# Keeping the masks of layer 0 on chip for layer 1 in a two-layer graph network kernel

## The chip, the cores and the metric

The kernel runs on one core of one Trainium2 chip. The metric is the device time of one execution in microseconds (us), the median of three runs. The core has five engines that run side by side and are tied together by semaphores: TensorE (in the profile PE, and PEld for its weight loads), VectorE (DVE), ScalarE (ACT), GpSimd (POOL) and SyncE (SP), which here only issues transfers. Sixteen DMA engines move the data that the queues of SP, ACT and POOL ask for.

## The reference

Sixteen graphs of 1024 nodes with 256 features each, and an adjacency matrix of integers (about 3% ones, ones on the diagonal). Layer 0 is masked attention with 8 heads of 32 features, layer 1 an attention over edge scores; both have a layer norm in front and a residual around them.

```python
# layer 0
h = jnp.maximum(_layernorm(x), 0.0)
Q, K, V = proj(Wq, bq), proj(Wk, bk), proj(Wv, bv)          # 8 heads of 32
scores = jnp.where(adj[:, None] == 0, -jnp.inf, Q @ K.T * SCALE)
x = x + (softmax(scores) @ V).reshape(b, n, 256) @ Wo.T + bo
# layer 1
h = jnp.maximum(_layernorm(x), 0.0)
scores = jnp.where(adj == 1, leaky_relu((h * a_0) @ h.T), NEG_INF)
...
scores = jnp.where(adj == 4, leaky_relu((h * a_3) @ h.T), scores)
x = x + softmax(scores) @ h
```

With the inputs drawn here adj holds only 0 and 1, so for layer 1 only a_0 matters. A path for other values (`layer_1_of_kinds`) stands at the end behind a test and isn't entered.

## The kernel before

A graph is worked through in 8 tiles of 128 query rows. The main loop (L710) runs over *steps*, one tile of layer 0 each: 128 tiles and ten more steps until the pipeline is empty. A step has 8 *slots*, one for each head (`h`, L713). In one step four tiles are under way:

- `now` (class `Attend`): the tile whose heads are scored. In slot h TensorE makes the scores (L402), VectorE adds the mask and takes the maximum in one pass (L414), ScalarE takes the exponential one slot later (L422), and the probabilities are turned two slots later. Odd heads are turned by TensorE and copied by ScalarE (L514, L515); even heads are turned by VectorE in blocks of 32 (L347), and four transfers of 128 KB on SP's queue put the blocks in place (L352).
- `was`: the tile before. In slot 3 `combine(1)` multiplies its heads 4 to 7 with the values (L457); heads 0 to 3 were done in slot 7 of its own step (`combine(0)`). Then output, residual, norm, and in slot 6 the result goes to DRAM (`keep`, L486).
- `edge`, `edge_was` (class `Edges`): a tile of layer 1 that lies `LAG` = 9 steps back. Scores in slots 0 and 1 (L543), maximum in slot 2 (L556), leak in 3 (L564), exponential in 4 (L568), blocks in 5 and 6, gathered (L584) and stored (L594) in the step after that.
- `piece`, `piece_was` (class `Piece`): a tile nine steps ahead, whose norm, queries, keys and values are made. Its keys go to DRAM twice: once on SP's queue as they are made (slots 0 and 1) and once on POOL's queue (`write_again`, slot 1, L297). At a change of graph the eight key tiles of the next graph, 512 KB each, are loaded on POOL's queue (`load_key`, L331), one in each slot from slot 3 of a graph's last step to slot 2 of the next graph's first.

Each engine and each queue works in the order in which the program writes its instructions; nothing is reordered. SP's order in a full step is: slot 0, keys of the piece, blocks of head 6 of the tile before; slot 1, keys, the next tile's adjacency (`Attend.load`, L376), its queries (L372); slot 2, blocks of head 0; slot 3, the next piece's nodes (L192) and the next edge tile's adjacency (`Edges.load`, L525); slot 4, blocks of head 2, and the residual of the edge tile (L572); slot 6, queries of the piece (L291), blocks of head 4, `keep`, the residual of the tile (`load_nodes`, L380), the edge tile's blocks; slot 7, the output.

POOL turns an adjacency tile into a mask of bf16 twice: for `Attend` (L384, slot 3) and, nine steps later, for `Edges` (L537, slot 7). Besides it has the chains of small operations of the norm (L144 to L160; slots 1 and 5), the spread reciprocals (L441, slot 1), the bias (L388, slot 2) and the scaled rows `ha` of layer 1 (L530, slot 4). ScalarE squares the adjacency tile in place once, to find whether it holds other kinds (`flag`, L393, slot 0).

The rows of an `Attend` tile are dealt to the partitions in another order than in DRAM (`mixed`, L341: row b*32+k lies on partition k*4+b), and those of an `Edges` tile in the order of DRAM. So `keep` stores through `mixed`, and `Edges` loads straight.

Of the kernel before, what the change touches and what calls it, by code (L numbers as in the profile page):

```python
# [17 lines left out]
P = 128  # L18
HEADS = 8
# [23 lines left out]
def gnn_kernel(  # L43
# [26 lines left out]
    LEAD = NT + 1  # L70

# [99 lines left out]
    class Piece:  # L171
# [5 lines left out]
        def __init__(self, b, first, n=1):  # L177
            self.b, self.first, self.n = b, first, n
            self.cols = slice(first * P, (first + n) * P)
            self.projected, self.halved, self.again = [], [], []  # L180
            self.tags = ("xin", "h0", "hT", "halves", "hTm") if n == 1 else ("adj", "pT", "qt", "p", "blocks")

        def buffer(self, i, shape, dtype=F32, bufs=2):
# [3 lines left out]
            bufs = {"p": 4, "blocks": 3}.get(tag, bufs)  # L187
# [75 lines left out]
        def high(self):  # L263
            which, oc, ps, bias = self.projected.pop(0)
            halves = self.buffer(3, [P, 2 * self.n * P], F32R, 4)
# [36 lines left out]
        def write_again(self):  # L302
            for oc, halves in self.again:
                self.write_keys(oc, halves, nc.gpsimd, 1)
# [39 lines left out]

    def blocks_of(p):
# [12 lines left out]
    h1s, h1Ts, x1ds = {}, {}, {}  # L358
    kinds_seen = const.tile([P, B * NT], F32, name="kinds_seen")

    class Attend:

# [11 lines left out]
        def load(self):  # L374
            self.adj = work.tile([P, N], I32, tag="adj")
            nc.sync.dma_start(out=self.adj, in_=mixed(adj[self.b, self.rows, :]))  # L376

        def load_nodes(self):
            self.xb = work.tile([P, D], F32, tag="xb")
            nc.sync.dma_start(out=self.xb, in_=mixed(x[self.b, self.rows, :]))  # L380

        def mask(self):
            self.neg = work.tile([P, N], BF16, tag="neg")
# [81 lines left out]
        def combined(self):  # L465
            self.oT = work.tile([P, NC, P], F32, tag="oT")
# [9 lines left out]
        def residual(self):  # L476
            self.x1 = work.tile([P, D], F32, tag="x1")
# [5 lines left out]
        def keep(self):  # L483
            if self.t == 0:
                x1ds[self.b] = dram.tile([N, D], F32, tag=f"x1d{self.b}", name=f"x1d_{self.b}", bufs=1)
            nc.sync.dma_start(out=mixed(x1ds[self.b][self.rows, :]), in_=self.x1)  # L486
# [31 lines left out]
    class Edges:  # L518
# [4 lines left out]
        def load(self):  # L523
            self.adj = work.tile([P, N], I32, tag="adj")
            nc.sync.dma_start(out=self.adj, in_=adj[self.b, self.rows, :])  # L525

        def prepare(self):
            self.ha = work.tile([P, NC, P], F32, tag="ha")
            for c in range(NC):
                nc.gpsimd.tensor_scalar(  # L530
                    self.ha[:, c], h1Ts[self.b][:, c, self.rows], a_t[:, c, 0:1], 0.0, ALU.mult, ALU.add
                )

        def mask(self):
            self.neg = work.tile([P, N], BF16, tag="neg1", bufs=1)

            nc.gpsimd.tensor_scalar(self.neg, self.adj, 0.0, MASKED, ALU.is_equal, ALU.mult)  # L537
# [14 lines left out]

        def softmax_max(self):
# [3 lines left out]
                out=self.sel, in0=self.e, in1=self.neg, scale=-1.0, scalar=3e38,  # L557
# [8 lines left out]
        def softmax_exp(self):  # L566
# [4 lines left out]
            self.x1 = work.tile([P, D], F32, tag="x1b")  # L571
# [17 lines left out]
        def store(self):  # L589
            rec = small.tile([P, 1], F32, tag="rec1")  # L590
            nc.vector.reciprocal(rec, self.total)
            ot = work.tile([P, D], F32, tag="ot")
            nc.vector.scalar_tensor_tensor(ot, sums_place, rec, self.x1, ALU.mult, ALU.add)  # L593
            nc.sync.dma_start(out=out[self.b, self.rows, :], in_=ot)  # L594


    def layer_1_of_kinds(b):
        h1 = graph.tile([P, NT, D], F32, tag="h1", name=f"h1g_{b}")
        h1T = graph.tile([P, NC, N], F32, tag="h1T", name=f"h1Tg_{b}")
        for t in range(NT):  # L600
            rows = slice(t * P, (t + 1) * P)
            xt = work.tile([P, D], F32, tag="x1")
            nc.sync.dma_start(out=xt, in_=x1ds[b][rows, :])
# [8 lines left out]
        for t in range(NT):  # L612
            rows = slice(t * P, (t + 1) * P)
            at = work.tile([P, N], I32, tag="adj")
            nc.sync.dma_start(out=at, in_=adj[b, rows, :])
            xt = work.tile([P, D], F32, tag="x1b")
            nc.sync.dma_start(out=xt, in_=x1ds[b][rows, :])

            code = work.tile([P, N], BF16, tag="neg1", bufs=1)
# [3 lines left out]
            for k in range(N_KINDS):  # L623
                ha = work.tile([P, NC, P], F32, tag="ha")
# [4 lines left out]
                is_k = work.tile([P, N], U16, tag="neg")  # L629
# [23 lines left out]
            ot = work.tile([P, D], F32, tag="ot")  # L653
# [20 lines left out]
    with tc.manual_schedule():  # L674
# [8 lines left out]
        now, piece_next = attend_of(0), piece_of(0)  # L683
        now.load()
        now.load_nodes()
        now.mask()
        piece_next.load()
# [22 lines left out]
        for s in range(B * NT + LAG + 1):  # L710
            b, t = divmod(s, NT)
            nxt, edge_nxt, piece_nxt = attend_of(s + 1), edges_of(s + 1), piece_of(s + 1)
            for h in range(HEADS):  # L713
# [41 lines left out]
                if h == 0:  # L755
                    if edge:
# [4 lines left out]
                    if now:  # L761
                        now.flag()
                if h == 1:
# [8 lines left out]
                    if nxt:  # L772
                        nxt.load()
# [8 lines left out]
                if h == 3:  # L782
                    if was:
                        was.combine(1)
                    if piece_nxt:
# [112 lines left out]
```

## Time and profile before

| | |
|---|---|
| median of 3 runs | 3405.14 us (3405.12 to 3412.75) |
| the profiled execution | 3404.83 us, its span 3403.0 us |
| TensorE clock granted, mean | 0.978 of full speed |
| moved by DMA | 830.24 MB, 244 GB/s over the span |
| transfers of blocks (L352) | 2560 of 128 KB, 3.3 us to landing (median) |
| adjacency loads (L376 and L525) | 256 of 512 KB, 5.3 us to landing |
| key loads on POOL's queue (L331) | 120 of 512 KB, 7.1 us to landing |
| POOL making masks | 128 x 3653 ns (L384) and 128 x 3659 ns (L537) |

How to read the lines that follow. A group shows line, engine, operation, output<-input, and how often. A line of waits reads "engine, line, what it waited for: us in total, times, longest". In the order of time the first two numbers are the start and the time until the end of the last of a run of equal instructions; in square brackets stands the idle time before and what ended it. SPq is SP's queue: its lines are issues of transfers, and their time is that of issuing. "To landing" runs from the issue of a transfer to the arrival of its last byte. A busy TensorE isn't TensorE at its peak, since ends of matmuls are modelled; idle time of an engine that isn't the bound costs nothing.

### The profile page before, as it was taken

The numbers are of one execution on the slowest core, as the hardware profiler recorded it, in microseconds if no ns is written. First come the engines' busy times: TensorE is split into PE (matmuls) and PEld (weight loads), VectorE is DVE, ScalarE is ACT, GpSimd is POOL, SyncE is SP. The second block draws the span as 40 slices with busy tenths as digits, with TensorE's granted clock in tenths as the row PEclk, the third lists the DMA queues.
The fourth block names the chain that finished last, engine by engine and source line by source line (L and its number), as shares of the span: only waits on it lengthen the run. The fifth ranks groups of instructions, "written<-read, shape, count | busy, mean of one in ns | idle before, by whom it ended". The sixth has DMA issues, their size and how long they took to land. (4 is left out here: it accounts for less than half of the span.)

```text
span 3403.0 us, 100938 instructions
## 1 busy us (share of the span) xinstructions
PE 3126.6 (92%) x36018; PEld 2247.9 (66%) x36018; DVE 2788.1 (82%) x5111; ACT 2418.2 (71%) x4829; POOL 2432.1 (71%) x5634
## 2 busy tenths in 40 slices
PE   5879989999999989999899999999999999998988
PEld 3666767666676767766666676767666676666653
DVE  3878888788888888888788788888888888788874
ACT  2887767677777777777777677777777677776751
POOL 2567777777777777777777777777777777776553
PEclk7999999999999999999999999999999999999999
DMA  6787788888888788788878888888788888888664
GB/s 221 211 249 241 234 268 249 268 239 245 265 241 277 236 268 247 237 271 248 267 231 250 265 236 282 240 270 248 234 268 249 267 235 251 267 238 261 196 175 113
DMA packets 802029, 830.24 MB, mean 244 GB/s; under 512 B 73840, under 2 KB 742640, under 8 KB 801520
## 3 DMA queue, kind: packets, MB, share of 16 engines
q1 hardware_dynamic: 769520, 725.10, 71.3%
q0 software_dynamic: 28800, 94.39, 7.9%
q8 instruction: 291, 4.77, 0.5%
q10 hardware_dynamic: 3200, 4.19, 0.3%
q14 instruction: 218, 1.79, 0.1%
HBM read 320.08 MB, written 167.77 MB: 143 GB/s over the span
## 5 line engine op out<-in xcount | busy, mean ns | idle before, releaser
L422 ACT ACTIVATE p<-p,nmx 128x1024 f32<-128x1024 f32 x1024 | 1179.2, 1152 | 454.9 <-DVE nmx L414 450.9
L414 DVE CUSTOM_DVE_ANT_0 p<-s,neg 128x1024 f32<-128x1024 f32 x1024 | 1242.1, 1213 | 207.2 <-PE s L402 195.8
L402 PE MATMUL s<-k,qt 128*128 128x512 f32 x2048 | 794.5, 469 | 41.3 <-DMA k<-kd 14.8
L457 PE MATMUL acc<-pT,v 128*32 128x128 f32 x16384 | 576.3, 283 | 140.2 <-DMA pT<-blocks 136.6
L515 ACT COPY pT<-trp 128x512 f32<-128x512 f32 x1024 | 542.5, 580 | 136.1 <-PE trp L514 134.6
L347 DVE STREAM_TRANSPOSE blocks<-p 128x1024 f32<-128x1024 f32 x512 | 634.8, 1240 | 0.0
L457 PEld LDWEIGHTS acc<-pT,v 128*32 128x32 f32 x16384 | 476.1, 113 | 213.6 <-issue 204.4
L514 PE MATMUL trp<-ident,p 128*128 128x128 f32 x4096 | 534.0, 274 | 2.1 <-ACT p L422 2.0
L514 PEld LDWEIGHTS trp<-ident,p 128*128 128x128 f32 x4096 | 480.7, 141 | 75.1 <-ACT p L422 6.9
L384 POOL TENSOR_SCALAR neg<-adj 128x1024 bf16<-128x1024 int32 x128 | 467.6, 3653 | 78.8 <-DMA adj<-in_adj 69.8
L584 PE MATMUL acc<-h,pT 128*32 128x256 f32 x8192 | 505.8, 383 | 6.2 <-DMA pT<-blocks 5.5
L537 POOL TENSOR_SCALAR neg<-adj 128x1024 bf16<-128x1024 int32 x128 | 468.4, 3659 | 39.0 <-DMA adj<-in_adj 29.0
L402 PEld LDWEIGHTS s<-k,qt 128*128 128x128 f32 x2048 | 328.9, 191 | 232.0 <-issue 136.6
L543 PE MATMUL s<-h1T,ha 128*128 128x512 f32 x1024 | 481.3, 593 | 0.5 <-ACT h1T L504 0.5
L584 PEld LDWEIGHTS acc<-h,pT 128*32 128x32 f32 x8192 | 244.0, 110 | 219.3 <-issue 73.2
L156 POOL TENSOR_SCALAR sq<-sq 128x1 f32<-128x1 f32 (+1 forms) x750 | 238.6, 318 | 65.5
L441 POOL COPY wide<-rec 128x256 f32<-128x256 f32 x128 | 51.1, 399 | 325.7 <-DVE rec L439 325.6
L543 PEld LDWEIGHTS s<-h1T,ha 128*128 128x128 f32 x1024 | 183.9, 190 | 141.1 <-issue 127.5
L556 DVE CUSTOM_DVE_ANT_0 sel<-s,neg 128x1024 f32<-128x1024 f32 x128 | 156.7, 1224 | 134.8 <-POOL ve L144 85.4
L157 POOL TENSOR_TENSOR r<-r,sq 128x1 f32<-128x1 f32 (+1 forms) x750 | 168.8, 225 | 62.6
L297 POOL DMA_DIRECT2D kd<-halves x240 | 176.6, 773 | 33.9 <-issue 24.3
L422 ACT ACTIVATION_READ_ACCUMULATOR p<-p,nmx 128x1 f32 x1024 | 198.7, 194 | 0.0
(103 smaller groups left out, 4096.6 us busy)
## 6 DMA issues: line engine op xcount, KB each, us to landing
pT<-blocks SPq DMA_DIRECT2D x2560, 128.0 KB, 3.3
adj<-in_adj SPq DMA_DIRECT2D x256, 512.0 KB, 5.3
qt<-qd SPq DMA_DIRECT2D x128, 512.0 KB, 5.9
qd<-halves SPq DMA_DIRECT2D x240, 256.0 KB, 3.3
k<-kd POOLq DMA_DIRECT2D x120, 512.0 KB, 7.1
kd<-halves SPq DMA_DIRECT2D x240, 128.0 KB, 2.3
kd<-halves POOLq DMA_DIRECT2D x240, 128.0 KB, 5.3
xb<-in_x SPq DMA_DIRECT2D x128, 128.0 KB, 2.5
```

Of the source, the lines that this page charges most:

```text
L156: g.tensor_scalar(sq, sq, 1.5, None, ALU.add)
L347: nc.vector.transpose(blocks.rearrange("p b j q -> p j b q"), p)
L384: nc.gpsimd.tensor_scalar(self.neg, self.adj, 0.0, MASKED, ALU.is_equal, ALU.mult)
L402: nc.tensor.matmul(self.ps[:, cols], lhsT=self.qt[:, h, :], rhs=keysets[self.b][h][:, cols], start=True, stop=True,)
L414: nc.vector.tensor_tensor_reduce(out=p, in0=sides[h in (3, 5, 7)], in1=self.neg, scale=-SCALE, scalar=FLOOR, op0=ALU.add, op1=ALU.min, acc ...
L422: nc.scalar.activation(p, p, AF.Exp, bias=nmx, scale=-1.0, accum_out=self.sums[:, h : h + 1])
L457: nc.tensor.matmul(sums_place[r * HD : (r + 1) * HD, g * P : (g + 1) * P], lhsT=vs[self.b][:, j, place_of(h) : place_of(h) + HD], rhs=self ...
L514: nc.tensor.transpose(tr[:, j, :], p[:, jj * P : (jj + 1) * P], ident)
L515: copy(pT[:, half * 4 : half * 4 + 4, :], tr)
L537: nc.gpsimd.tensor_scalar(self.neg, self.adj, 0.0, MASKED, ALU.is_equal, ALU.mult)
L543: nc.tensor.matmul(self.e[:, cols], lhsT=self.ha[:, c, :], rhs=h1Ts[self.b][:, c, cols], start=(c == 0), stop=(c == NC - 1),)
L584: nc.tensor.matmul(sums_place[a * HD : (a + 1) * HD, :], lhsT=self.pT[:, j, a], rhs=h1s[self.b][:, j, :], start=(j == 0), stop=(j == NT - 1),)
```

## The change

Layer 1's tile of the same rows uses the mask that layer 0 made. Masks live in ten buffers (`KEPT` = `LAG` + 1) and are found through a dictionary; `Edges.load` and `Edges.mask` are gone. For that, layer 1 takes its rows in the mixed order too: `ha` is read from `h1T` through a permuted view, `keep` now stores straight, and the output is stored through `mixed`. Most other work tiles get one buffer instead of two, among them adj, the residual xb, ha, x1, oT, ot and the piece's tiles.

Several calls change place in the step. The adjacency of a tile is loaded two steps ahead, in slot 7 (it was one step ahead, in slot 1). The flag moves from slot 0 of a tile's own step to slot 6 of the step before. The piece's nodes are loaded in slot 5 instead of 3; the edge tile's residual in slot 0 of the step after, instead of slot 4; the residual of a tile in slot 6 of its own step, where that of the next tile was loaded in slot 6 for its use a step later. The keys' second write goes out one at a time, in slots 0 and 1. The eight key loads lie in slots 2, 3, 5 and 6 of the last step of a graph and 0, 1, 3 and 4 of the first of the next.

```diff
+    KEY_STEPS = (2, 3, 5, 6, 8, 9, 11, 12)
+    KEPT = LAG + 1
...
-            self.tags = ("xin", "h0", "hT", "halves", "hTm") if n == 1 else ("adj", "pT", "qt", "p", "blocks")
+            self.tags = ("xin", "h0", "hT", "halves", "hTm") if n == 1 else ("pT", "pT", "qt", "p", "blocks")
...
-            bufs = {"p": 4, "blocks": 3}.get(tag, bufs)
+            bufs = {"p": 4, "blocks": 3, "halves": 4, "qt": 2}.get(tag, 1)
...
         def write_again(self):
-            for oc, halves in self.again:
+            while self.again:
+                oc, halves = self.again.pop(0)
                 self.write_keys(oc, halves, nc.gpsimd, 1)
...
         def load(self):
-            self.adj = work.tile([P, N], I32, tag="adj")
+            self.adj = work.tile([P, N], I32, tag="adj", bufs=1)
...
         def mask(self):
-            self.neg = work.tile([P, N], BF16, tag="neg")
+            self.neg = work.tile([P, N], BF16, tag="neg", bufs=KEPT)
+            masks[self.b, self.t] = self.neg
...
-            nc.sync.dma_start(out=mixed(x1ds[self.b][self.rows, :]), in_=self.x1)
+            nc.sync.dma_start(out=x1ds[self.b][self.rows, :], in_=self.x1)
...
-        def load(self):
-            self.adj = work.tile([P, N], I32, tag="adj")
-            nc.sync.dma_start(out=self.adj, in_=adj[self.b, self.rows, :])
...
-                    self.ha[:, c], h1Ts[self.b][:, c, self.rows], a_t[:, c, 0:1], 0.0, ALU.mult, ALU.add
+                    self.ha[:, c].rearrange("p (k b) -> p k b", b=NB),
+                    h1Ts[self.b][:, c, self.rows].rearrange("p (b k) -> p k b", b=NB),
+                    a_t[:, c, 0:1], 0.0, ALU.mult, ALU.add,
...
-        def mask(self):
-            self.neg = work.tile([P, N], BF16, tag="neg1", bufs=1)
-
-            nc.gpsimd.tensor_scalar(self.neg, self.adj, 0.0, MASKED, ALU.is_equal, ALU.mult)
...
-                out=self.sel, in0=self.e, in1=self.neg, scale=-1.0, scalar=3e38,
+                out=self.sel, in0=self.e, in1=masks[self.b, self.t], scale=-1.0, scalar=3e38,
...
-            nc.sync.dma_start(out=out[self.b, self.rows, :], in_=ot)
+            nc.sync.dma_start(out=mixed(out[self.b, self.rows, :]), in_=ot)
...
+        nxt = attend_of(1)
         now.load()
-        now.load_nodes()
         now.mask()
+        now.flag()
+        nxt.load()
         piece_next.load()
...
                 if h == 0:
+                    if piece_was:
+                        piece_was.write_again()
...
-                    if now:
-                        now.flag()
+                    if edge_was:
+                        edge_was.load_nodes()
                 if h == 1:
...
                     if nxt:
-                        nxt.load()
                         nxt.load_queries()
...
                 if h == 3:
...
-                    if piece_nxt:
-                        piece_nxt.load()
-                    if edge_nxt:
-                        edge_nxt.load()
...
                 if h == 5:
...
+                    if piece_nxt:
+                        piece_nxt.load()
...
                 if h == 6:
...
+                    if now:
+                        now.load_nodes()
                     if nxt:
-                        nxt.load_nodes()
+                        nxt.flag()
...
                 if h == 7:
...
-                    if edge_nxt:
-                        edge_nxt.mask()
+                    if nxt2:
+                        nxt2.load()
...
-                if now and h >= 3 and t == NT - 1 and b + 1 < B:
-                    load_key(b + 1, h - 3)
-                if now and h < 3 and t == 0 and b > 0:
-                    load_key(b, HEADS - 3 + h)
-            gone, was, now = was, now, nxt
+                if now and t == NT - 1 and b + 1 < B and h in KEY_STEPS:
+                    load_key(b + 1, KEY_STEPS.index(h))
+                if now and t == 0 and b > 0 and HEADS + h in KEY_STEPS:
+                    load_key(b, KEY_STEPS.index(HEADS + h))
+            gone, was, now, nxt = was, now, nxt, nxt2
```

## The prediction

> **What bounds the kernel now.** I read the page's busy shares first, then the sums of waits, then the order of time of one step of the main loop on every engine, then the length of each step.
>
> ```profile
> PE 3126.6 (92%) x36018; PEld 2247.9 (66%) x36018; DVE 2788.1 (82%) x5111; ACT 2418.2 (71%) x4829; POOL 2432.1 (71%) x5634
> POOL neg L537 <- DMA adj<-in_adj: 29.0, 6, 8.4
> PE acc L457 <- DMA pT<-blocks: 136.6, 111, 5.3
> PE s L402 <- DMA k<-kd: 14.8, 12, 2.9
> ```
>
> TensorE is the bound: of its 276 us without work, half is one wait, for the turned probabilities (pT<-blocks). POOL, where the change takes 128 x 3659 ns = 468 us away (L537), is idle for 971 us, so that saving is worth only what waits for POOL: `sel` waits for `neg` 10.6 us in all, 5 times.
>
> I took the distance from one transpose of the reciprocals (L447, once a step) to the next as the length of a step. In the 84 steps inside a graph, once the pipeline is full, it has a median of 24.47 and a mean of 24.62 us; the two steps around a change of graph take 26.44 and 30.06 (means of 14). So a change of graph costs 7.6 us, 15 times: 113 us.
>
> Inside a graph the step is held by a place where two chains meet. Order of time, three engines:
>
> ```profile
> 1002.40 2.54 SPq L352 DMA_DIRECT2D pT<-blocks  x4
> 1007.47 2.49 SPq L352 DMA_DIRECT2D pT<-blocks  x4
> 1010.06 0.55 SPq L594 DMA_DIRECT2D out<-ot  x1
> 1010.70 0.55 SPq L297 DMA_DIRECT2D kd<-halves  x1
> 1011.34 2.53 SPq L352 DMA_DIRECT2D pT<-blocks  x4
> 1014.60 0.41 PE L457 MATMUL acc<-pT,v 128*32 128x128 f32 x4
> 1015.97 1.94 PE L457 MATMUL acc<-pT,v 128*32 128x128 f32 x60 [0.96 <-DMA pT<-blocks]
> 1017.70 0.41 DVE L326 TENSOR_TENSOR v<-acc,bv_t 128x256 f32<-128x256 f32 x1
> ```
>
> Read from above: SP issues the blocks of head 4 as soon as VectorE has turned them, then without a pause the store and load of slot 6, the edge's blocks, `out`, the keys (kd), and the blocks of head 6. At 1014.60 TensorE has done heads 4 and 5 of combine(1) and stands until head 6's blocks are there. A step later that stand is 0.16 us, but the next product then waits 0.39 for DVE `v`: VectorE's chain from the edge's scores to `v` is the floor under the step. Taking the span of combine(1) less the 1.95 us that it needs as the gap g, the steps obey length = 24.46 + max(0, g - 1.21): g of 1.47, 1.73, 2.44 go with 24.71, 25.00, 25.69. The mean g inside graphs is 1.04. **So head 6's blocks have 0.2 us to spare, and whatever delays them further is paid in every step.**
>
> **The parts, and their cost.**
>
> *The mask load moves ahead of head 6's blocks.* The next adj load (L376) was issued in slot 1, after these blocks; it is now issued in slot 7, between `out` and kd in the SP row above. No other transfer leaves the stretch between head 4's and head 6's blocks: `keep` and the load of xb (L380) stay, and turning `out` into a mixed store and `keep` into a straight one swaps 0.55 against 0.60 us of issue. So SP gets there one issue later: 0.58 + 0.07 between issues = 0.65 us. The 512 KB of the mask then travel ahead of the blocks. These landing times are of head 6's blocks now, of head 0's blocks issued 1.3 us after adj and 0.65 after qt, and of all adj loads of L376:
>
> ```profile
> DMA to landing us min/median/max: 2.5/2.6/2.6
> DMA to landing us min/median/max: 5.1/6.0/6.2
> DMA to landing us min/median/max: 3.9/4.7/7.9
> ```
>
> Two loads of 512 KB ahead cost the last block 2.5 us (5.1 against 2.6). One load might cost all of one half, 1.25, plus up to 0.25 from the POOL write of keys that also moves to slot 0; so at most 1.5. At least it costs 0: the DMA share is only 0.69 and 0.74 in the two 5 us stretches around that place, and the blocks are issued one by one over 2.5 us, so the load may have passed. An estimate in between: served in order, head 0's last block lands 8.3 us after adj is issued (1.3 + 1.9 + 5.1) with twelve pieces of 128 KB done, say 2.3 to start and 0.5 each; nine pieces (adj, kd, blocks) then take 6.8, against 1.3 + 1.9 + 2.6 = 5.8 undisturbed, so 1.0. I take 0.7, near the middle of the ends. New g: 1.04 + 0.65 + 0.7 = 2.39; length 24.46 + 1.18 = 25.64, **1.02 more than 24.62**. Over 84 steps: 86 us. The 15 steps before a change of graph pay the same: 15. The first seven and the last six steps, with fewer transfers in that row but gaps of their own (0.8 to 1.8 in the last), I put at 1 us each: 13, between 0 and 20.
>
> [...]
>
> *The edge's own mask and load go.* L525 and L537 are off the path inside graphs: SP issues L525 in slot 3, when it waits for VectorE anyway. In the last nine steps, without attention, SP's blocks and TensorE end the waits. The one place there where DVE waits long for POOL (5.89 us, at 3315.50) has TensorE's scores ending at 3315.29, so 0.2 is to be had, and 0.9 of a 2.09 us leak (1.18 elsewhere): -1. Bounds 0 and -10.6.
>
> *Keys over ten slots.* POOL issues them in its program order, and two now stand behind long work. At the change of graph at 1675 the row is: reciprocals at 1675.36, the rest of the norm to 1681.7, one write of keys 0.73, then key 5 at 1682.4; bias, mask 3.65, key 6 at 1687.8; two ha, key 7 at 1689.2. Median landing is 7.2, so they are there at 1689.6, 1695.0 and 1696.4. Key 5 is wanted at 1689.5 now. Of the gap of about 6 us there I take 0.9 off: 0.65 of issue is added, but 0.5 MB net less lies ahead (key 5 behind, the edge's mask gone, the moved mask added), at 340 GB/s 1.5 us. Then key 5 stalls 1.0, key 6 1.7 (wanted 3.7 after 5), key 7 nothing: +1.8 for each change, 15 times: 27. Bounds: -75 (the 30.06 falls to about 25), if the burst alone makes that gap, and +81 with the longest landing, 10.8.
>
> *The flag* (L393, 1.15 + 0.19 on ACT) moves from slot 0 to slot 6 and now needs the mask of the same step. POOL ends that mask at 1023.46; it begins 0.73 earlier since one key write has left for slot 0. ACT reaches the flag at about 1025, after the exponential of slot 6, so 2.3 us are to spare; behind it the exponential of head 6 comes 0.4 late and the copies after it had waited 1.15 for TensorE. If that cover went, ACT's queue (that exponential, copies of turned probabilities) would stand. Before the loop there is none: the flag now precedes the first copies of turned nodes (L227, at 33.27), and the mask ends at 36.47: 36.47 + 1.34 + a little - 33.27 = **4 us later**, and TensorE's first projections with it. Bounds 0 and 6.
>
> *One buffer each.* The reloads stand behind work long done: xin in slot 5 behind the norm of slot 4, x1 in slot 0 behind the store of slot 7, xb in slot 6 behind the residual of slot 5, and ha, oT, hT, x1 and ot are a whole step apart. The tightest is xin: issued after head 2's blocks, at 1023.6, 2.8 to 5.3 us to land, read by DVE at 1028.8. The tenfold `neg` buffer lets the new mask wait for the edge's maximum of slot 2, at 1013 against a mask at 1019. Nothing taken. The strided ha (L530, 375 ns twice) I take at no cost: ACT's permuting copy L236 takes 400 ns against 378 straight, and even double would be 0.75 us on POOL.
>
> "Trainium Kernel Development and Optimization", Best Practices, asks for double buffers under DMA, which speaks against the change. In this trace no single buffer's release by itself ends a wait; what the missing second buffer does is to fix the slot of the load.
>
> **Sum**, against the profiled 3403.0: 86 + 15 + 13 + 27 + 4 - 1 = 144, 3547 of span. The run that was profiled lists 3404.8, the median 3405.1, so 2 are added: **3549 us**, 4.2% more. With the term of the moved load at its ends alone (0 and 1.5) it is 3472 (a length of 24.94) and 3635 (26.44); that is the range of this case.
>
> **Rivals.**
>
> *The moved load is nearly free and the changes of graph are cured.* Around the change of graph shown, the DMA engines are full for some 35 us; in these stretches of 5 us the DMA share and the GB/s stand last:
>
> ```profile
> 1665.00:1670.00 5.00, 5.00 (x85) 4.17 (x85) 3.20 (x9) 2.78 (x8) 3.78 (x18) 1.00 1.00 327
> 1675.00:1680.00 5.00, 3.49 (x26) 2.87 (x26) 4.70 (x8) 3.77 (x8) 4.04 (x14) 1.00 1.03 348
> 1680.00:1685.00 5.00, 1.02 (x20) 1.05 (x24) 1.11 (x2) 2.92 (x6) 4.51 (x12) 0.84 1.00 344
> ```
>
> Less to move and a longer stretch for the keys bear on just this. With only the issue paid, inside graphs 0.32 x 84 = 27, and 9 elsewhere and 4 at the start, against -75 -15: 3355. It decides if the load delays the blocks by under 0.3 us and keys 5 and 6 land in time. Against it: keys 5 to 7 go out no earlier than worked out above. Chance 0.24.
>
> *Late keys are the main loss*: the load free (27 + 9 + 4), the keys at their longest landing (81): 3526. For it: TensorE waits for keys now already. Against: only 14.8 us of it. Chance 0.17.
>
> *Gains and losses cancel*, within 0.3% (about what a measurement of this kernel can tell from no change): 0.06. My forecast: 0.53.
>
> The range is 3365 to 3635: it leaves out the better half of the first rival and the worst of the forecast. Faster by over 0.3% 0.24, within 0.06, slower 0.70.
>
> **What would show it.** Step length 25 to 26.3 inside graphs, with a gap of 2 to 3 us before combine(1)'s third head in nearly all of them; landing of head 6's blocks 3 to 4 us; waits for `k` at heads 5 and 6 after a change of graph; first projection at about 41 us. Wrong, if steps stay at 24.5: then the blocks had room that I missed.

## The result, and the profile after

The changed kernel takes 3605.76 us (median of 4 runs, 3589.0 to 3620.97), the kernel before 3408.94 in the same comparison: **slower by 5.7%**, ratio 1.0572 with an interval of 1.0518 to 1.0625. The profiled execution, the slowest of the four, took 3620.97 us; its span is 3619.2 against 3403.0, and the mean granted clock of TensorE is 0.950 against 0.978. In the names below, lines are those of the changed kernel, about ten higher than before (combine is L468, was L457).

The page, engines and DMA:

```profile
PE 3188.2 (88%) x36018; PEld 2334.5 (65%) x36018; DVE 2793.6 (77%) x5111; ACT 2449.1 (68%) x4829; POOL 1997.3 (55%) x5506
...
DMA packets 783597, 763.12 MB, mean 211 GB/s; under 512 B 71792, under 2 KB 740592, under 8 KB 783088
```

The saving is there as written: POOL has 128 instructions and 435 us less to do, and 67 MB (128 loads of 512 KB) are gone. TensorE is busy 61.6 us longer with the same 36018 matmuls; nothing in the change touches their sizes. Sums of TensorE's waits:

```profile
PE acc L468 <- DMA pT<-blocks: 314.5, 127, 5.7
...
PE s L413 <- DMA k<-kd: 12.3, 12, 2.3
```

The wait for the turned blocks was 136.6 and is 314.5; the wait for keys has not grown (14.8, now 12.3). SP in order of time, one step inside a graph (start, time until the last issue ends):

```profile
986.46 2.50 SPq L361 DMA_DIRECT2D pT<-blocks  x4
989.06 0.60 SPq L601 DMA_DIRECT2D out<-ot  x1
989.76 0.56 SPq L386 DMA_DIRECT2D adj<-in_adj  x1
990.41 0.56 SPq L301 DMA_DIRECT2D kd<-halves  x1
991.06 2.54 SPq L361 DMA_DIRECT2D pT<-blocks  x4
```

The adjacency stands between `out` and kd, 0.65 us until the next issue. These four blocks of head 6 then take longer, too. Issue to landing in that last stretch:

```profile
DMA to landing us min/median/max: 3.5/4.0/4.4
```

Over the 84 steps inside graphs the block issued first takes 3.92 us (median) and the one issued last 3.28, where they took 2.54 and 2.61. TensorE needs all four, so it is the last that ends its pause: 0.67 us later by its data. TensorE at that place, then the same place a few steps later:

```profile
993.97 0.41 PE L468 MATMUL acc<-pT,v 128*32 128x128 f32 x4
996.51 2.89 PE L468 MATMUL acc<-pT,v 128*32 128x128 f32 x60 [2.12 <-DMA pT<-blocks]
...
1103.40 0.41 PE L468 MATMUL acc<-pT,v 128*32 128x128 f32 x4
1105.42 1.94 PE L468 MATMUL acc<-pT,v 128*32 128x128 f32 x60 [1.60 <-DMA pT<-blocks]
```

Both pauses are what the forecast was about. But after the longer one the same 60 matmuls take 2.89 us and not 1.94. Three stretches of 3.41 us from that pause on tell why (columns: stretch, its length, busy time of PE, PEld, DVE, ACT, POOL, then the granted clock, the DMA share and GB/s):

```profile
993.91:997.32 3.41, 1.29 (x38) 0.96 (x40) 3.41 (x5) 2.20 (x5) 2.59 (x9) 1.00 0.85 266
997.32:1000.73 3.41, 3.41 (x44) 2.82 (x33) 0.71 (x3) 2.77 (x5) 3.32 (x3) 0.50 0.94 297
1000.73:1004.15 3.42, 3.42 (x28) 2.96 (x30) 3.35 (x7) 2.00 (x4) 2.75 (x4) 1.00 0.07 25
```

The granted clock is 0.50 for one stretch of 3.41 us, which begins 0.8 us after TensorE starts again, and is 1.00 before and after it.

Measured as in the prediction, from one transpose of the reciprocals (now L458) to the next, the step inside graphs is 26.66 us in the mean (24.62 before). In 46 of the 84 steps combine(1) runs slowed as in the first of the two places (its last 60 matmuls take over 2.2 us, 3.25 in the mean); these steps take 27.64 us. The other 38 take 25.48. The difference is not the clock alone: the pause is 2.47 us in the mean of the 46 and 1.94 in that of the 38. So the table takes the two losses apart by another way. The delay is what the step law of the prediction gives for each step's pause; the clock's part is the time by which the last 60 matmuls run over 1.94 us. The two add up to the loss but for 1 us, and the second is near the 61.6 us that TensorE is busy longer.

| where | span, us more than before |
|---|---|
| 84 steps inside graphs: 84 x 2.04 | 171 |
| of these, delay, by the step law from the pauses (0.65 us in the mean before, 2.23 after) | 110 |
| of these, the slowed clock: 46 x (3.25 - 1.94) | 60 |
| two steps around a change of graph: 14 x (0.26 + 0.48) | 10 |
| first eight intervals / last seven | 13 / 19 |
| start, end of the program | 2, 0.4 |
| all, against 216.2 of span | 215 |

### The profile page after: what moved, and what is told of

Its sections match the earlier page's. It is cut to its first block, busy times and chain, and to the rows that moved or that the text cites. A ratio compares the mean times of both kernels' runs of the same rounds, so it can differ in the third digit from the quotient of the medians.

```text
span 3619.2 us, 100887 instructions
## 1 busy us (share of the span) xinstructions
PE 3188.2 (88%) x36018; PEld 2334.5 (65%) x36018; DVE 2793.6 (77%) x5111; ACT 2449.1 (68%) x4829; POOL 1997.3 (55%) x5506
## 5 line engine op out<-in xcount | busy, mean ns | idle before, releaser
L468 PE MATMUL acc<-pT,v 128*32 128x128 f32 x16384 | 653.4, 306 | 318.8 <-DMA pT<-blocks 314.5
L413 PE MATMUL s<-k,qt 128*128 128x512 f32 x2048 | 809.3, 477 | 37.4 <-DVE nmx L425 19.6
L468 PEld LDWEIGHTS acc<-pT,v 128*32 128x32 f32 x16384 | 541.7, 123 | 396.6 <-issue 275.7
L395 POOL TENSOR_SCALAR neg<-adj 128x1024 bf16<-128x1024 int32 x128 | 470.3, 3674 | 40.5 <-DMA adj<-in_adj 25.4
L160 POOL TENSOR_SCALAR sq<-sq 128x1 f32<-128x1 f32 (+1 forms) x750 | 265.5, 354 | 65.5
L478 DVE TENSOR_TENSOR oT<-acc,recT 128x256 f32<-128x256 f32 x128 | 54.2, 423 | 235.8 <-PE acc L468 213.4
L515 ACT COPY h1T<-acc 128x256 f32<-128x256 f32 x128 | 47.7, 373 | 214.2 <-PE acc L511 214.1
```

Of the source, the lines that this page charges most:

```text
L160: g.tensor_scalar(sq, sq, 1.5, None, ALU.add)
L413: nc.tensor.matmul(self.ps[:, cols], lhsT=self.qt[:, h, :], rhs=keysets[self.b][h][:, cols], start=True, stop=True,)
L468: nc.tensor.matmul(sums_place[r * HD : (r + 1) * HD, g * P : (g + 1) * P], lhsT=vs[self.b][:, j, place_of(h) : place_of(h) + HD], rhs=self ...
```

## The experiments

The theory: the moved load delays head 6's blocks twice, by its issue on SP and by its data, and the pause that this makes also costs TensorE its clock. The rivals: late keys; the rest of the change (masks kept, single buffers, mixed order); a pure delay, with the clock as a mere sign of it.

In the table, step is the mean over the 84 steps inside graphs, "slowed" the number of them in which combine(1) runs slowed; the last two columns are TensorE's waits for blocks and for keys.

| kernel | median us | ratio to before, 95% | step | slowed | blocks | keys |
|---|---|---|---|---|---|---|
| before | 3400 to 3409 | | 24.62 | 0 | 136.6 | 14.8 |
| after | 3605.8 | 1.0572 (1.0518 to 1.0625) | 26.66 | 46 | 314.5 | 12.3 |
| e1, load behind | 3442.8 | 1.0134 (1.0092 to 1.0177) | 24.56 | 1 | 138.4 | 63.0 |
| e2, before with the load ahead | 3653.9 | 1.0740 (1.0707 to 1.0773) | 26.96 | 49 | 323.3 | 7.7 |
| e3, a quarter ahead | 3535.7 | 1.0392 (1.0354 to 1.0431) | 25.35 | 13 | 221.8 | 56.7 |
| e4, filler | 3548.0 | 1.0428 (1.0379 to 1.0477) | 26.05 | 9 | 213.7 | 17.2 |
| e5, e1 with keys in eight slots | 3397.5 | 0.9977 (0.9961 to 0.9994) | 24.60 | 1 | 160.7 | 18.6 |
| e6, e1 with keys earlier | 3416.5 | 1.0037 (1.0016 to 1.0057) | 24.69 | 2 | 198.6 | 0.6 |
| e7, load ahead on ACT's queue | 3463.0 | 1.0168 (1.0115 to 1.0221) | 25.33 | 13 | 213.6 | 20.6 |
| e8, before with ten slots | 3470.1 | 1.0189 (1.0142 to 1.0236) | 24.61 | 0 | 85.9 | 96.0 |
| e9, e1 with keys on ACT's queue | 3389.3 | 0.9943 (0.9924 to 0.9962) | 24.59 | 1 | 110.7 | 1.3 |
| e10, e9 with stores behind | 3335.4 | 0.9800 (0.9786 to 0.9815) | 24.37 | 0 | 13.7 | 7.3 |
| e11, after with stores behind | 3408.3 | 1.0022 (1.0008 to 1.0036) | 24.55 | 0 | 156.6 | 24.0 |
| e12, e10 with three keys on ACT | 3359.2 | 0.9875 (0.9857 to 0.9893) | 24.38 | 0 | 31.0 | 16.3 |

### The load alone, undone and done

**e1** is the change with the adjacency load back in slot 1, one step ahead.

```diff
+                    if nxt and s > 0:
+                        nxt.load()
                     if nxt:
                         nxt.load_queries()
...
-                    if nxt2:
-                        nxt2.load()
```

> The changed kernel with one part undone: a tile's adjacency is loaded in slot 1 of the step before, behind head 6's blocks, as it was; everything else as changed. Theory (the moved load delays head 6's blocks, and the longer pause lets the clock of TensorE drop): steps inside a graph fall from 26.7 to 24.5-24.7 us, no step with combine(1) at the low clock inside a graph, time about 3619 - 84 x 2.05 - 15 (first) - 18 (last) - 25 = 3390, between 3360 and 3420. Rival (late keys after a change of graph): 3560 to 3610. Rival (single buffers or the flag in slot 6): above 3500.

The loss falls from 5.7 to 1.3%, with 3443 us a little above the 3360 to 3420 expected. The step is 24.56 us, at the length of before, and one step of 84 is slowed. What is left is at the changes of graph: their two steps take 25.29 and 33.25 us (26.44 and 30.06 before), and 14 x (33.25 - 30.06 - 1.15) is 28.6 of the 29.6 us that the span is longer than before. The same two waits:

```profile
PE acc L468 <- DMA pT<-blocks: 138.4, 106, 4.3
PE s L413 <- DMA k<-kd: 63.0, 28, 5.5
```

The blocks are back where they were; the keys, quiet in the changed kernel, cost 63 us. That is the rival of late keys, and it comes up only once the steps are short. At one change of graph, POOL and TensorE in order of time:

```profile
2106.27 3.65 POOL L395 TENSOR_SCALAR neg<-adj 128x1024 bf16<-128x1024 int32 x1 [6.55 <-DMA adj<-in_adj]
...
2115.26 1.22 PE L413 MATMUL s<-k,qt 128*128 128x512 f32 x2 [5.51 <-DMA k<-kd]
```

POOL waits 6.55 us for the adjacency, the mask follows, and the next key load stands behind both; TensorE pays 5.51. In all, the masks of e1 wait 142.1 us for their adjacency, 80 times. In the changed kernel, where the load has a step more, that was 25.4 us, 6 times.

**e2** is the kernel before with nothing but the load two steps ahead in slot 7 (and the flag after it, as the buffer needs it).

```diff
-                    if now:
-                        now.flag()
...
-                        nxt.load()
                         nxt.load_queries()
...
                         nxt.load_nodes()
+                        nxt.flag()
...
                         edge_nxt.mask()
+                    if nxt2:
+                        nxt2.load()
```

> The kernel before with one part of the change alone: the flag in slot 6 and the adjacency loaded two steps ahead in slot 7; both mask loads, both mask passes, two buffers, keys in eight slots as before. Theory: steps inside a graph 26 to 27.5 us, time 3560 to 3640. Rivals (late keys; single buffers): within 0.5% of before, 3390 to 3425.

7.4% slower, more than the whole change and than the 3560 to 3640 expected. In 49 of 84 steps combine(1) runs slowed, after a pause of 2.54 us in the mean; those take 27.93 us and the others 25.59. The wait is the one of after:

```profile
PE acc L457 <- DMA pT<-blocks: 323.3, 128, 6.9
```

So one moved load is enough for the loss, and the rest of the change isn't needed for it. The flag, which moves with it, isn't the cause: in e1 it stands in slot 6 as well.

### Issue or data

**e3** loads a quarter of the columns ahead and the rest in slot 1: the issue is paid in full, a quarter of the data travels ahead. **e7** takes the load off SP's queue but leaves its slot: the data travel ahead, SP issues nothing for them.

```diff
 # e3
-            nc.sync.dma_start(out=self.adj, in_=mixed(adj[self.b, self.rows, :]))
+            nc.sync.dma_start(
+                out=self.adj[:, : N // 4], in_=mixed(adj[self.b, self.rows, : N // 4])
+            )
+
+        def load_rest(self):
+            nc.sync.dma_start(
+                out=self.adj[:, N // 4 :], in_=mixed(adj[self.b, self.rows, N // 4 :])
+            )
...
                     if nxt:
+                        nxt.load_rest()
                         nxt.load_queries()
 # e7
-            nc.sync.dma_start(out=self.adj, in_=mixed(adj[self.b, self.rows, :]))
+            nc.scalar.dma_start(out=self.adj, in_=mixed(adj[self.b, self.rows, :]))
```

> The changed kernel with the adjacency load split: a quarter of the columns (128 KB) in slot 7, the rest (384 KB) in slot 1 of the next step behind head 6's blocks. SP still issues one transfer more ahead of the blocks. If the issue alone were the cause: as the changed kernel, 3590 to 3620. If the 512 KB of data alone: near the kernel with the load behind, about 3400. My terms (0.65 issue, 0.7 or more data) give 24.46 + 1.04 + 0.65 + 0.2 - 1.21 = 24.9 us per step and 3430 to 3470.

> The changed kernel with the adjacency load in slot 7 as changed, but issued on ACT's queue: the data go ahead of head 6's blocks, SP's issue (0.65 us) doesn't. Theory with both terms: of the 1.5 to 1.6 us that the blocks come later, 0.65 go; steps without a slow clock 25.0 to 25.2 and fewer of the others, time 3470 to 3540. If the data cost nothing: 3420 to 3445. If the issue costs nothing: 3590 to 3620.

TensorE's pause before head 6's products, in the mean of the 84 steps, is 0.65 us in before, 1.43 in e3 and 2.23 in after. So the issue with a quarter of the data adds 0.78 us, and the other three quarters of the data add 0.80. **Both terms are real**, and neither explains the other away. e3's landing of head 6's blocks is 2.5 to 2.7 us again, as before, so a quarter of the data no longer delays them, and its 0.78 us are nearly all the issue's.

e7 doesn't leave the data term alone, as it was meant to. ACT reaches the load earlier than SP did: it is issued 7.25 us before the first of head 6's blocks (median; 1.30 in after). These blocks then travel as in before (from the last issue to TensorE's start 2.91 us in the mean, 2.82 in before, 3.54 in after). SP issues them 0.77 us later than in before, counted from TensorE's first four products, and that makes the pause of 1.51 us. A wait that after hardly has stands in SP's row ahead of them, that of `out` for turned blocks (SPq L601 <- DMA pT<-blocks: 40.3 us, 54 times; in after 1.9, twice). So a load issued earlier on another queue delays the blocks too, by another way, which was not followed further.

The time of e3, 3536, is above what was expected: thirteen steps are slowed all the same (27.45 us each), and TensorE waits for the keys as in e1, since the mask waits for the rest of its adjacency:

```profile
PE acc L475 <- DMA pT<-blocks: 221.8, 117, 6.1
PE s L420 <- DMA k<-kd: 56.7, 24, 6.0
```

The second of the two steps around a change of graph is 34.9 us there (30.5 in after). e7, 3463, came a little below its range.

### The clock

**e4** leaves all delays of the change in place and gives TensorE two products of 0.5 us, whose result nobody reads, just before combine(1).

```diff
                     if was:
+                        for _ in range(2):
+                            nc.tensor.matmul(
+                                late, lhsT=woT[:, 0, :P], rhs=woT[:, 1, :], start=True, stop=True
+                            )
                         was.combine(1)
```

> The changed kernel with two matmuls added ahead of combine(1) whose result nobody reads (128x256, about 1 us in all), which lie in the pause. Theory that TensorE's clock drops after a pause of some 2 us and costs about 1.4 us in half of the steps: pause 1.0 to 1.5, combine(1) at 1.94 us nearly everywhere inside graphs, steps 25.6, time 3530 to 3570. If the slow combine(1) has nothing to do with the pause: same or slower, 3600 to 3700.

Slowed steps fall from 46 to 9, and the time by 58 us to 3548, with more work on the engine that bounds the kernel. Inside graphs the 84 steps take 51 us less, and the last 60 matmuls of combine(1), over their 1.94 us, 50 us less. TensorE in order of time:

```profile
1026.39 1.03 PE L795 MATMUL acc<-woT 128*128 128x256 f32 x4
1027.35 0.41 PE L468 MATMUL acc<-pT,v 128*32 128x128 f32 x4
1029.56 1.94 PE L468 MATMUL acc<-pT,v 128*32 128x128 f32 x60 [1.80 <-DMA pT<-blocks]
```

The filler changes nothing on SP or in the transfers; it takes part of the pause (1.48 us in the mean of the 84 steps, 2.23 in after), and combine(1) mostly runs at its 1.94. A pure delay would have left the time where it was. So the clock is a loss of its own.

How long may the pause be? Over all 14 profiles, wherever TensorE idles at least 0.15 us just before the last 60 matmuls of combine(1), I set this pause against whether they took over 2.2 us:

| pause before combine(1)'s last 60, us | slowed |
|---|---|
| under 1.75 | 2 of 957 |
| 1.75 to 2.0 | 24 of 91 |
| 2.0 to 2.5 | 91 of 142 |
| 2.5 to 3.5 | 99 of 126 |
| over 3.5 | 118 of 119 |

What decides in between is where the pause lies. In the clock's record of all 14 profiles the granted clock is 1.00 or 0.50 and nothing else; within a profile the falls to 0.50 all begin on one grid of 3.413 us, and they last one window of this grid or several, but for one at the very end of each. From 250 us after the start to 130 us before the end, TensorE's busy time in a window with the clock at 1.00, set against the clock in the window behind it:

| TensorE busy in one window of 3.413 us | clock 0.50 in the next window |
|---|---|
| under 1.3 us | 298 of 298 |
| 1.3 to 1.6 | 116 of 166 |
| over 1.6 | 1 of 11612 |

So a pause costs the clock when some 2 us of it lie in one window. That of 2.12 us shown above does (1.29 us busy). One of 3.27 us in after, from 2036.60 to 2039.88, is cut by the end of a window at 2038.39; TensorE is busy 1.62 and 1.92 us in the two windows, and the clock stays at 1.00.

### The keys

**e8** puts the ten slots alone into the kernel before, **e5** puts eight neighbouring slots into e1.

```diff
 # e8 (in before)
+    KEY_STEPS = (2, 3, 5, 6, 8, 9, 11, 12)
...
-                if now and h >= 3 and t == NT - 1 and b + 1 < B:
-                    load_key(b + 1, h - 3)
-                if now and h < 3 and t == 0 and b > 0:
-                    load_key(b, HEADS - 3 + h)
+                if now and t == NT - 1 and b + 1 < B and h in KEY_STEPS:
+                    load_key(b + 1, KEY_STEPS.index(h))
+                if now and t == 0 and b > 0 and HEADS + h in KEY_STEPS:
+                    load_key(b, KEY_STEPS.index(HEADS + h))
 # e5 (in e1)
-    KEY_STEPS = (2, 3, 5, 6, 8, 9, 11, 12)
+    KEY_STEPS = (3, 4, 5, 6, 7, 8, 9, 10)
```

> The kernel before with the keys in the ten slots of the change, nothing else. Theory: keys 5 to 7 are late as in the kernel with the load behind, more so, since POOL still has the edge's mask: wait for k 50 to 100 us, time 3430 to 3480. If spreading helps the DMA engines more than it delays the keys: 3370 to 3400.

> The changed kernel with the adjacency load behind head 6's blocks (slot 1), and the keys in eight slots in a row, as before. Theory (what keeps the kernel with the load behind 1.3% above before is keys 5 to 7, which stand on POOL behind the norm and behind a mask that waits for its adjacency): the wait for k falls from 63 to 10-25 us, the long step at a change of graph from 33.3 to 29-30.5, time 3375 to 3400, 0 to 1% below before. Rival (the rest is from single buffers, the permuted views or the start): 3420 to 3445.

e8 is 1.9% slower. Its two waits trade places:

```profile
PE s L403 <- DMA k<-kd: 96.0, 40, 6.9
PE acc L458 <- DMA pT<-blocks: 85.9, 99, 3.9
```

The wait for blocks falls (136.6 before, 85.9 now; the gap g of the prediction, in the step at a change of graph, from 6.35 to 0.91; where the clock falls in combine(1), its slowing is counted in g here and below), and the keys that the spread puts behind POOL's norm and mask cost more than that. Little of the fall is load taken off the blocks, since the last of head 6's four blocks still takes 5.9 us to land there (median; 6.2 in before): TensorE, held up by the keys, comes later. In e5 the wait for keys falls from 63.0 to 18.6 and the time to 3397, 0.2% under the kernel before. So the rest of the change, the kept masks with it, is worth 0.2% with the load and the keys in their old places, and that is hardly clear of its interval (0.9961 to 0.9994).

**e6** issues the first five keys of e1 in neighbouring slots, 2 to 6, and keys 5 and 6 in slot 1 ahead of what POOL has to do there. **e9** takes the keys from 2 on off POOL and gives them to ACT's queue.

```diff
 # e6 (in e1)
+    KEY_STEPS = (2, 3, 4, 5, 6, None, None, 10)
...
+                    if now and t == 0 and b > 0:
+                        load_key(b, 5)
+                        load_key(b, 6)
 # e9 (in e1)
-        (nc.sync, nc.gpsimd)[b > 0].dma_start(
+        (nc.sync if b == 0 else nc.gpsimd if h < 2 else nc.scalar).dma_start(
```

> The changed kernel with the adjacency load in slot 1, and keys 0 to 4 in slots 2 to 6 of a graph's last step, keys 5 and 6 in slot 1 of the next step ahead of the norm, key 7 in slot 2 ahead of the mask. Theory: no key stands behind mask or norm, and none goes out just ahead of head 6's blocks, so the gap there falls from 6 to some 3-4 us as well: long step 27.5 to 29, time 3350 to 3385. If the gap is made by DMA load whatever the order: 30 us a long step, 3385 to 3400.

> The changed kernel with the adjacency load in slot 1, the keys in the ten slots of the change, but keys 2 to 7 issued on ACT's queue instead of POOL's, so that they go out in their slots and not behind the norm and the mask. Theory (the spreading is right for the DMA engines, and only POOL's lag makes keys 5 to 7 late): wait for k under 15 us, long step 27 to 29, time 3340 to 3380. If the gap before head 6's blocks comes from DMA load however it is spread: long step 30 to 31, 3385 to 3405.

e6 misses: the keys are in time, but the wait for blocks rises to 198.6, and the gap g in the step at a change of graph from 4.72 in e1 to 7.75 (6.35 before). At one of them POOL issues keys 5 and 6, 1 MB, from 1678.16 to 1679.23, SP the blocks from 1679.63 on, and TensorE waits 6.21 us for these. That the keys delay them is read from this order and wasn't tried apart. e9, 3389, misses its 3340 to 3380 and lies by its time in the rival's range, but not for the rival's reason: the keys are in time, the gap at a change of graph is 1.42, and a new wait stands in its place. TensorE's waits:

```profile
PE acc L468 <- DMA pT<-blocks: 110.7, 106, 3.4
PE trp L525 <- ACT p L433: 56.4, 15, 6.0
```

Fifteen times, once for each change of graph, TensorE waits for ScalarE, whose exponentials stand behind the key issues.

### Clearing SP's row

**e10** is e9 with `keep` and the residual's load moved from between the blocks of heads 4 and 6 to behind the latter. **e11** is that move alone in the changed kernel, load still ahead.

```diff
+                    if gone:
+                        gone.keep()
+                    if was:
+                        was.load_nodes()
...
-                    if was:
-                        was.keep()
-                    if now:
-                        now.load_nodes()
```

> As the run with keys on ACT's queue, and besides the store of the tile and the load of its residual (two transfers of 128 KB, about 1.3 us of issue on SP) moved from slot 6 to slot 0, behind head 6's blocks. Theory (whatever stands on SP between head 4's and head 6's blocks is paid or gained there): the gap falls by about 1.3 us in every step; inside graphs it is hidden already but for the steps above 24.4, so 24.6 falls to 24.4 (about 15 us in all), and 1 to 1.3 us at each change of graph: 25 to 40 us below the run with keys on ACT's queue. If SP's order no longer matters: the same time.

> The changed kernel, adjacency load still in slot 7 ahead of head 6's blocks and keys as changed, but the tile's store and its residual load moved from slot 6 to slot 0, behind the blocks. SP then issues one transfer fewer ahead of the blocks than before the change. Theory (the position of the blocks in SP's order is what counts, and 1.3 us taken off pays back 1.3 us per step and most of the drops of the clock): steps inside a graph 24.6 to 25.1, few or none with combine(1) at the low clock, late keys remain; time 3440 to 3490. If the data of the load were the main cost: 3540 to 3600.

e10 takes **3335 us, 2.0% less than before** and 54 us less than e9, where 25 to 40 were expected. Its row on SP, and TensorE's largest waits:

```profile
1019.33 0.60 SPq L601 DMA_DIRECT2D out<-ot  x1
1020.03 0.56 SPq L301 DMA_DIRECT2D kd<-halves  x1
1020.75 2.52 SPq L361 DMA_DIRECT2D pT<-blocks  x4
1023.32 0.59 SPq L579 DMA_DIRECT2D x<-x1d  x1
1023.96 0.46 SPq L497 DMA_DIRECT2D x1d<-x  x1
1024.52 0.55 SPq L390 DMA_DIRECT2D xb<-in_x  x1
```

```profile
PE acc L257 <- DVE v L331: 70.9, 94, 0.9
PE trp L525 <- ACT p L433: 44.9, 22, 4.3
...
PE acc L468 <- DMA pT<-blocks: 13.7, 23, 2.7
```

The wait for blocks, 110.7 in e9, is 13.7: the step is no longer held there but by VectorE's `v`, in 94 short waits, and its 24.37 us are near the floor of 24.46 that the prediction read from `v`. e11 is better than expected: with the adjacency still ahead, the two issues saved bring the step to 24.55 and no step is slowed, although the blocks take 3.3 to 4.2 us to land (medians of the last and the first). 3408 us is 0.2% over the kernel before: to take 1.15 us of issue (0.46 and 0.55, and 0.07 behind each) and 256 KB out of this row brings back nearly all that the change lost.

**e12** is e10 with only the last three keys on ACT's queue, to relieve ScalarE.

```diff
-        (nc.sync if b == 0 else nc.gpsimd if h < 2 else nc.scalar).dma_start(
+        (nc.sync if b == 0 else nc.gpsimd if h < 5 else nc.scalar).dma_start(
```

> As the fastest so far (adjacency in slot 1, store and residual load in slot 0, keys in ten slots), but only keys 5 to 7 on ACT's queue, 0 to 4 on POOL's. In the run with six keys on ACT, key 5 held ACT for 3.2 us and key 6 for 2.2 us. If these waits come from the earlier key loads on ACT's own queue: wait of the turned products for the exponential falls from 45 to under 15 us, time 3300 to 3325. If not: 3330 to 3350.

The wait for the exponential falls, but the time is 3359, 0.7% above e10 and outside both ranges:

```profile
PE acc L468 <- DMA pT<-blocks: 31.0, 30, 3.6
...
PE trp L525 <- ACT p L433: 16.8, 15, 3.0
PE s L413 <- DMA k<-kd: 16.3, 19, 2.5
```

28.1 us less of waiting for ScalarE stand against 17.3 more for blocks and 9.0 more for keys, besides longer steps at the changes of graph (the gap there 2.55 against 0.92). What held the exponentials in e10 I read from ScalarE's order of time there:

```profile
1250.64 0.33 ACTq L336 DMA_DIRECT2D k<-kd  x1
1251.07 1.15 ACT L433 ACTIVATE p<-p,nmx 128x1024 f32<-128x1024 f32 x1 [3.19 <-DMA kd<-halves]
```

The key's load waits for the keys' second write (kd<-halves) to land, and ScalarE stands 3.19 us with it. Which of the transfers ahead made that write late was not tried.

## Why the prediction was right

**The direction and the chain.** The forecast named the moved load, head 6's blocks and the wait at combine(1), and gave 3549 us in 3365 to 3635; 3605.76 lies in it. e1 and e2 show that this one move is both needed and enough for the loss.

**The sum of the moved load.** Issue: 0.65 us, as measured. Data: 0.7 taken, 0.67 measured at the last block, which ends the pause. Pause: 1.35 us more were forecast, 1.58 measured; issue and data leave some 0.25 us of it unexplained. Delay: 86 us were forecast in the 84 steps, 110 come out of the measured pauses. The 38 steps that keep the clock take 25.48 us, against 25.64 forecast, but they are those with the shorter pauses, so their nearness tests little. e3 confirms that both the issue and the data are paid.

**The mis-sized term** is "Over 84 steps: 86 us". It priced the pause as delay alone, and the clock that the pause costs at nothing. The 84 steps lost 171 us: 110 of delay, and 60 because in 46 of them the last 60 matmuls of combine(1) take 3.25 us in the mean and not 1.94. That the time still lies in the range is in part luck: its upper end, 3635, was there for a data term of 1.5 us, and the clock used up that room. The profile of before had the warning: in the row 1680 to 1685 that the prediction itself shows, the clock is 0.84 in the mean after a long gap, and combine(1) there takes 3.32 us. I read that row for its transfers only. The prediction put the mean gap at 2.39, of which the first four matmuls of combine(1) are 0.4; that is a pause of 2.0 us, past the 1.75 from which the table of pauses has slowed steps.

The Trainium skill's "TensorE: Matmul & The Clock Gate", section "Why this matters for your kernels", advises against idle gaps of TensorE of over about 3 us between bursts, since one idle window halves the clock. These runs agree that the clock falls behind a pause and that it halves (0.50 in the row above), but not on the limit: pauses of 2.0 to 2.5 us are enough in 91 of 142 cases. By the page's limit, the pause of 2.12 us shown above would have kept its clock.

**The first and last steps**, 13 forecast, cost 32 (13 at the head, 19 at the tail). The tail was put at 1 us a step and took 2.7: its mean pause before head 6's products went from 0.83 to 2.75 us. No experiment took it apart by itself.

**Changes of graph**: 15 + 27 forecast, 10 measured. Of the 15, only 4 show: in the step before the change of graph the pause grew from 0.76 to 2.31 us, but waits that made this step long before, 0.82 us for keys above all, are gone there. The 27 for late keys weren't paid in this kernel either. When TensorE is on time, keys 5 to 7 are late, and by more than was worked out (96.0 us of waiting in e8, 63.0 in e1). In the changed kernel TensorE comes later itself, and the mask seldom waits for its adjacency (25.4 us in all, 142.1 in e1), so the delay of POOL's queue is hidden; that is read from the waits, not tried. The rival "late keys are the main loss" is thus a real mechanism that the larger one covered. The rival "the changes of graph are cured" fell as argued: in e8 and e1 they pay in keys what they save in blocks.

**Start, single buffers, edge masks.** The first projection starts at 41.5 us, as forecast (about 41), after 37.1; of these 4 us only 2.0 are left at the first transpose of the reciprocals. No release of a single buffer shows among the long waits, and e11, with all of them, is within 0.2% of the kernel before. The permuted `ha` costs more than "nothing": 497 ns each against 375, 0.24 us a step on POOL, which has room.

```profile
L537 POOL TENSOR_SCALAR ha<-h1T,a_t 128x128 f32<-128x128 f32 x256 | 124.9, 497 | 61.8 <-PE s L547 51.9
```

## What to carry to other kernels

Before a transfer is moved ahead on a queue, find what the transfers behind it feed and how much slack that has: here it was 0.2 us in a step of 24.6, and 67 MB less to load and 435 us off POOL could not make up for one issue in the wrong place. A pause of the engine that bounds the kernel is to be priced twice, as delay and as the clock that it may cost afterwards; look up in the trace of before what the clock did behind its longest pauses. A saving off the critical path becomes worth something only when the row that holds the step is cleared: the change was worth 0.2% with the load and the keys where they had been (e5), and 2.0% with the keys on another queue and two more issues behind the critical blocks (e10). How much of the 2.0% these two moves would give the kernel before, without the kept masks, was not tried.

## What the runs showed of the hardware that had not been expected

The clock falls behind pauses much shorter than the steps they stand in: almost never below 1.75 us (2 of 957), mostly above 2.0, nearly always above 3.5 (118 of 119). The granted clock is then 0.50 for 3.41 us, and the 60 small matmuls take 2.4 to 3.6 us and not 1.94. It is the busy time of TensorE in each window of 3.413 us that goes with it, 298 falls of 298 under 1.3 us and 1 of 11612 over 1.6, so of two equal pauses the one that lies across the end of a window can be free. The filler cost TensorE about 1 us a step and still saved 58 us.

A transfer of 512 KB issued 1.3 us ahead delays the 128 KB blocks behind it by 1.4 us (the first, 2.54 to 3.92) down to 0.7 (the last, 2.61 to 3.28), a quarter of it by less than 0.1 (2.55 and 2.69).
